# A new order for the pieces of v, q and k in a two-layer graph kernel, and a start rearranged around the graph's turning

The kernel runs on one core of a Trainium2 chip. The metric is the device time of one execution in microseconds (us).

## The reference, cut to what matters

There are 32 graphs with 512 nodes and 512 features each. All share one 0/1 adjacency matrix `adj` of 512 x 512.

```python
# layer 0
a, deg = adj.astype(x.dtype), adj.sum(axis=1)
out = deg[None, :, None] * (x @ Wi.T + b) + a @ (x @ Wj.T)
x = layernorm(x + out)
# layer 1: 8 heads of 64, scores masked where adj == 0
q, k, v = heads(x @ Wq.T + bq), heads(x @ Wk.T + bk), heads(x @ Wv.T + bv)
attn = softmax(where(adj == 0, -inf, q @ k.T / 8))
x = layernorm(x + merge(attn @ v) @ Wo.T + bo)
```

## The kernel before

The products named here are fp32. Each 512 x 512 product is made with seven quarter-size products in place of eight, called *pieces*. The pieces fall into three groups, {1, 2}, {6, 7, 4} and {5, 3}; those of a group add up in one PSUM tile of one bank. There are two such banks for the pieces, `mma` and `mmb`, with one buffer each. After every piece another engine reads the tile out (an *eviction*), so the next piece on that bank must wait for the eviction:

```python
    def piece(kind, b, i, bank):
        g = GROUP[i]
        first = (kind, b, g) not in OPEN
        if first:
            OPEN[kind, b, g] = mm_tile(bank)
        pm = OPEN[kind, b, g]
        # ... 8 matmuls (16 in layer 0) from a ring of weight blocks into pm
        prefetch()
        if i == 1:
            p1 = OPEN[kind, b, "p1"] = work([P, 2, Q], "p1", 3)
            nc.scalar.copy(p1, pm)                              # L363
        # ...
        elif kind == "v":
            if i == 2:
                nc.scalar.copy(d, pm)
            elif i in (6, 7, 4):
                nc.vector.tensor_tensor(d, pm, p1, op=OP.add)   # L382
            elif i != 1:
                nc.vector.tensor_tensor(d, d, pm, op=OP.add)    # L384
        # ... q and k likewise, L390 (two rows at once) and L399 (two parts)
```

The order of the pieces of one graph in layer 1 is a list, in which v runs on bank a, q on bank b and k on bank a:

```python
        res += [norm[0], norm[1], z(apply, n, 1), pc("v", n, 1, "a"), pc("q", n, 1, "b")]
        # ...
        res += [norm[2], norm[3], z(combos, TH, n, h, (1, 2)), pc("v", n, 2, "a"), pc("q", n, 2, "b"),
                pc("k", n, 1, "a"), z(combos, TH, n, h, (3, 4)), z(add_bo, n, 0), z(add_bo, n, 1), pc("k", n, 2, "a")]
        # ...
        for i in ORDER[2:]:                       # 6, 7, 4, 5, 3
            res += [pc("v", n, i, "a"), pc("q", n, i, "b")]
```

`combos` makes sums of quarters of the activations on GpSimd. A period (one for each graph) is this list together with layer 0 of the next graph and the attention of the graph before, cut into 8 steps. Each step begins with `scores` and `values` and, in every second step, `sums`; then its share of the pieces follows. The partial sums of the exponentials (`presum`) go out behind the first piece of a step:

```python
            late = [(presum, hp, half)]           # half 0: GpSimd, half 1: two adds on VectorE (L422)
            for f in PERIODS[n][step]:
                # ... run(f), then late and a share of the softmax's remaining work
            for g in late + extra:
                g[0](*g[1:])
```

The weights' own sums are made once, at the start, by `combine`; they are written to DRAM, from where the ring of 12 blocks reads them:

```python
    combine("wj", nc.gpsimd)
    combine("wi", nc.vector)
    prefetch()
    for f in PERIODS[0]:
        run(f)
```

`fold` puts the bias of v, times Wo, into the bias of the output: 8 matmuls, in the middle of the first period.

## Time and profile before

| | before |
|---|---|
| time, median of 3 runs | 4021.6 us (4021.29 to 4022.62) |
| span of the profiled execution | 4021.7 us |
| TensorE busy | 3876.8 us (96%) |
| length of a steady period | 122.53 us |
| graph's last block cast, first piece, first scores | 10.99, 46.02, 143.20 us |

The start, timeline of the kernel before (columns: start in us, duration in us, engine, line and operation, output <- input, shape, count; in brackets the idle time just before and what ended it):

```profile
10.99 0.43 DVE L149 CAST big<-big 128x512 f32<-128x512 int32 x1 [0.52 <-DMA big<-in_adj_dram]
...
46.02 3.62 PE L356 MATMUL mma<-ring,big 128*128 128x256 f32 x16
52.66 6.61 PE L356 MATMUL mmb<-ring,big 128*128 128x256 f32 x16 [3.02 <-POOL big L325]
...
143.20 1.99 PE L408 MATMUL sc<-q,k 64*128 64x512 f32 x8
```

The cast is when the graph has arrived in full, the second line the first piece of layer 0, the last the first scores, at which the steady schedule begins. The third shows TensorE at its lower clock: 16 matmuls take 6.61 us there, at a mean granted clock of 0.56, and 3.62 us one line above.

### The profile page before, as it was taken

What the parts mean: (1) busy time and instruction counts of PE and PEld (TensorE: products, weight loads), DVE (VectorE), ACT (ScalarE), POOL (GpSimd) and SP (SyncE); (2) the same over time, 40 slices, a digit from 0 to 9 for tenths busy, and PEclk for the clock granted to TensorE, in tenths of its full rate; (3) what the DMA queues carried; (4) which work ended last, traced back from release to release, by engine and by line L of the source; (5) the groups of instructions that cost most, each with busy time, mean ns of one, the idle gap of its engine ahead of it and who ended that gap; (6) DMA issues with size and microseconds to landing.
All of it is one profiled execution on the core that took longest, in us unless ns stands there. A gap on an engine that the chain in (4) does not pass through costs nothing.

```text
span 4021.7 us, 47158 instructions
## 1 busy us (share of the span) xinstructions
PE 3876.8 (96%) x17418; PEld 2655.3 (66%) x17418; DVE 2608.9 (65%) x3524; ACT 1059.7 (26%) x1483; POOL 1851.6 (46%) x1866
## 2 busy tenths in 40 slices
PE   6999999999999999999999999999999999999997
PEld 4766666666666666666666666666666666666663
DVE  4466666666666666666666666666666666676666
ACT  1212222222222223222222222232222222222222
POOL 3445445445345454454453454444444534544432
PEclk8999999999999999999999999999999999999998
DMA  7333343333333333333333333333333334333330
GB/s 251 103 99 106 108 121 100 103 108 110 110 115 92 113 108 103 122 100 103 108 113 108 118 89 112 109 107 116 105 98 113 107 110 118 95 106 112 105 107 22
DMA packets 284346, 437.55 MB, mean 109 GB/s; under 512 B 23248, under 2 KB 121040, under 8 KB 284112
## 3 DMA queue, kind: packets, MB, share of 16 engines
q1 hardware_dynamic: 283856, 433.94, 35.9%
q8 instruction: 142, 2.33, 0.2%
q0 software_dynamic: 256, 0.53, 0.1%
q14 instruction: 92, 0.75, 0.1%
HBM read 392.96 MB, written 41.42 MB: 108 GB/s over the span
## 4 chain that ended last, share of the span: by engine, by line
PE 81%; DVE 14%; issue 3%; ACT 1%; POOL 1%; DMA 0%; SPq 0%; POOLq 0%; ACTq 0%; DVEq 0%
PE mma L356 32%; PE mmb L356 17%; PE sc L408 10%; PE ov L430 10%; PE mmb L280 6%; DVE xh L293 5%; DVE rl L443 3%; PE ov L437 2%; DVE es L422 2%; DVE e L413 2%; PE sc L273 1%; PE sc L301 1%; DVE ov L448 1%; ACT big L302 0%; ACT p L363 0%
## 5 line engine op out<-in xcount | busy, mean ns | idle before, releaser
L356 PE MATMUL mma<-ring,big 128*128 128x256 f32 x5288 | 1228.1, 382 | 47.3 <-issue 29.3
L356 PEld LDWEIGHTS mma<-ring,big 128*128 128x128 f32 x5288 | 991.6, 190 | 236.4 <-issue 66.3
L412 ACT ACTIVATE sc<-sc 128x1024 f32<-128x1024 f32 x512 | 492.8, 1006 | 1563.2 <-PE sc L408 1562.1
L413 DVE TENSOR_TENSOR e<-sc,edge 128x1024 f32<-128x1024 f32 x512 | 602.4, 1217 | 355.9 <-ACT sc L412 355.9
L419 POOL TENSOR_TENSOR es<-e 128x1024 f32<-128x1024 f32 x128 | 301.0, 2352 | 778.4 <-PE ov L437 778.4
L325 POOL TENSOR_TENSOR big<-big 128x512 f32<-128x512 f32 x384 | 525.0, 1390 | 236.5 <-DVE big L274 196.8
L408 PE MATMUL sc<-q,k 64*128 64x512 f32 x2048 | 509.7, 616 | 0.2 <-ACT big L302 0.2
L430 PE MATMUL ov<-e,v 128*64 128x512 f32 x2048 | 497.5, 607 | 6.5 <-DVE told L448 6.5
L443 DVE RECIPROCAL rl<-ov 128x128 f32<-128x128 f32 x512 | 458.7, 927 | 5.4 <-PE ov L437 1.6
L356 PE MATMUL mma<-big,ring 128*128 128x256 f32 x1792 | 430.2, 383 | 24.6 <-ACT p L363 20.9
L248 POOL TENSOR_SCALAR mv<-mv 128x1 f32<-128x1 f32 x256 | 79.2, 309 | 774.6 <-DVE mv L247 759.8
L356 PE MATMUL mmb<-big,ring 128*128 128x256 f32 x1792 | 432.6, 384 | 0.0
L356 PEld LDWEIGHTS mmb<-big,ring 128*128 128x128 f32 x1792 | 333.1, 190 | 113.9 <-issue 47.9
L356 PEld LDWEIGHTS mma<-big,ring 128*128 128x128 f32 x1792 | 334.8, 190 | 110.5 <-ACT p L363 33.4
L430 PEld LDWEIGHTS ov<-e,v 128*64 128x64 f32 x2048 | 124.7, 136 | 347.5 <-issue 272.8
L422 DVE TENSOR_TENSOR es<-es,e 128x1024 f32<-128x1024 f32 x256 | 313.5, 1225 | 4.4
L408 PEld LDWEIGHTS sc<-q,k 64*128 64x128 f32 x2048 | 176.5, 186 | 209.4 <-issue 195.8
L371 POOL TENSOR_TENSOR xh<-xh,p 128x512 f32<-128x512 f32 x189 | 235.5, 1274 | 104.5 <-ACT p L363 103.8
L374 DVE TENSOR_TENSOR xh<-xh,mma 128x512 f32<-128x512 f32 x189 | 127.8, 676 | 232.4 <-PE mma L356 232.4
L356 PE MATMUL mmb<-ring,big 128*128 128x256 f32 x1080 | 267.3, 392 | 10.7 <-POOL big L325 8.0
L183 POOL TENSOR_TENSOR xlo<-xh,xhi 128x512 fp32r<-128x512 f32 x128 | 162.6, 1281 | 220.8 <-ACT xhi L182 220.7
L356 PEld LDWEIGHTS mmb<-ring,big 128*128 128x128 f32 x1080 | 203.9, 194 | 90.7 <-POOL big L325 33.1
(109 smaller groups left out, 3667.0 us busy)
## 6 DMA issues: line engine op xcount, KB each, us to landing
ring<-wi SPq DMA_DIRECT2D x160, 256.0 KB, 2.6
ring<-wj SPq DMA_DIRECT2D x160, 256.0 KB, 2.8
ring<-wv SPq DMA_DIRECT2D x160, 256.0 KB, 2.7
ring<-wq SPq DMA_DIRECT2D x160, 256.0 KB, 2.7
ring<-wk SPq DMA_DIRECT2D x160, 256.0 KB, 4.4
ring<-wo SPq DMA_DIRECT2D x155, 256.0 KB, 2.6
xh<-in_x_dram SPq DMA_DIRECT2D x32, 1024.0 KB, 5.5
out_dram<-xh SPq DMA_DIRECT2D x31, 1024.0 KB, 5.1
```

The lines of the kernel that those rows point to most:

```text
L280: nc.tensor.matmul(pm, parts[w][:, jc, :], adjR[:, jc, :], start=(w == 0 and jc == 0), stop=(w == 1 and jc == NC - 1))
L293: nc.vector.scalar_tensor_tensor(y, b0_r, deg_c[:, ic:ic + 1], y, op0=OP.mult, op1=OP.add)
L325: nc.gpsimd.tensor_tensor(dst, p, q, op=OP.subtract)
L356: nc.tensor.matmul(pm[:, c * Q:(c + 1) * Q], lhs, rhs, start=first, stop=(kc == 1 and n == len(terms) - 1), skip_group_check=True)
L371: nc.gpsimd.tensor_tensor(d, d, p1, op=OP.add)
L408: nc.tensor.matmul(ps[:, s, :], KT[b, hp // 2][r, hp % 2, kc * P:(kc + 1) * P], QT[b, hp // 2][r, hp % 2, :], start=True, stop=True)
L412: nc.scalar.activation(ps, ps, AF.Exp, scale=QSCALE)
L413: nc.vector.tensor_tensor(e, ps, edge[:, kc:kc + 1, :].to_broadcast([P, 2, N]), op=OP.mult)
L419: nc.gpsimd.tensor_add(ES[hp], E[0], E[1])
L422: nc.vector.tensor_add(ES[hp], ES[hp], E[kc])
L430: nc.tensor.matmul(PV[hp][s * HD:(s + 1) * HD, :], V[b][:, kc, c0:c0 + HD], E[kc][:, s, :], start=(kc == 0), stop=(kc == NC - 1))
L443: nc.vector.reciprocal(rl[:, c], pl[:, c])
```

## The change

It intends two things. First, v, q and k get an order in which no piece follows one on its own bank, so that every eviction has a piece on the other bank to hide behind. Secondly, the start is rearranged: the weights' loads go behind the turning (transposing) of the graph, on ScalarE's queue, those of wi, wj and wk in halves; `combine` is split in parts that are placed among the first graph's work; `fold` moves to the end of the first period. The bias adds of the output (`add_bo`) also move to other places in a period. Not in the cut below: the first two graphs get another order of the pieces of layer 0 (their second and third change places), and the work that makes the masks from the graph (`graph_forms`) is split in three. The core of the diff:

```diff
-    combine("wj", nc.gpsimd)
-    combine("wi", nc.vector)
-    prefetch()
-
-    for f in PERIODS[0]:
+    for i, f in enumerate(PERIODS[0]):
+        if f[1] is piece and ring.used == 0:
+            load_w(wo, woT, nc.scalar)
+            W["wo"] = [wo[:, 0:2, :], wo[:, 2:4, :]]
+            load_x(1)
+            prefetch()
         run(f)
...
-    def combine(name, eng):
+    def combine(name, eng, part):
...
-        nc.scalar.mul(n22, a22, -1.0)
+            eng.tensor_scalar(n22, a22, -1.0, 1.0, op0=OP.mult, op1=OP.mult)
...
+            if n == 0 and i == 0:
+                res += [z(combine, "wj", nc.gpsimd, 0)]
+            if n == 0 and i == 2:
+                res += [z(combine, "wi", nc.vector, 0), z(combine, "wi", nc.vector, 1)]
...
+        if n == 0:
+            res += [z(combine, "wj", nc.gpsimd, 1)]
+        if n == 1:
+            res += [z(fold)]
...
-        res += [norm[2], norm[3], z(combos, TH, n, h, (1, 2)), pc("v", n, 2, "a"), pc("q", n, 2, "b"),
-                pc("k", n, 1, "a"), z(combos, TH, n, h, (3, 4)), z(add_bo, n, 0), z(add_bo, n, 1), pc("k", n, 2, "a")]
+        res += [pc("v", n, 2, "a"), norm[2], norm[3], z(combos, TH, n, h, (1, 2)), pc("k", n, 1, "a"),
+                z(combos, TH, n, h, (3, 4)), pc("q", n, 2, "b"), pc("k", n, 2, "a")]
...
-            res += [pc("v", n, i, "a"), pc("q", n, i, "b")]
+            res += [pc("q", n, i, "b"), pc("v", n, i, "a")]
```

More of the change, by code (lines that the diff above doesn't have):

```diff
@@ L128, in gnn_attention_kernel, with load_halves @@
     load_x(0)
+    W = {}
+    def load_halves(name, src, tag, eng):
+        W[name] = [work([P, 2, D], tag, 3) for _ in range(2)]
+        for j in range(2):
+            eng.dma_start(W[name][j], rows(src)[:, 2 * j:2 * j + 2, :])
     ident = const.tile([P, P], FT, name="ident")
@@ L134, in gnn_attention_kernel @@
     nc.gpsimd.memset(mhalf, -0.5)
-    W = {}
-    W["wj"] = load_w(big(), wjT, nc.sync)
-    W["wi"] = load_w(big(), wiT, nc.sync)
-    W["wv"] = load_w(work([P, NC, D], "v", 2), wvT, nc.sync)
-    W["wq"] = load_w(work([P, NC, D], "v", 2), wqT, nc.sync)
     b0_r = load_row("b0_r", b0)
@@ L159, in gnn_attention_kernel @@
     adjT = turned(adj_f, big())
-    W["wk"] = load_w(big(), wkT, nc.sync)
-    W["wo"] = load_w(wo, woT, nc.sync)
-    load_x(1)
+    load_halves("wi", wiT, "k", nc.scalar)
+    load_halves("wj", wjT, "oT", nc.scalar)
     deg_r = const.tile([P, N], FT, name="deg_r")
@@ L191, in gnn_attention_kernel, with graph_forms @@
     ahead(0)
+    for name, src in (("wv", wvT), ("wq", wqT)):
+        t = load_w(work([P, NC, D], "v", 2), src, nc.scalar)
+        W[name] = [t[:, 0:2, :], t[:, 2:4, :]]
+    load_halves("wk", wkT, "q", nc.scalar)
     edge = const.tile([P, NC, N], BF, name="edge")
-    def graph_forms():
-        nc.vector.tensor_tensor(adj_f, adjT, adjR.bitcast(FT), op=OP.not_equal)
-        nc.vector.reduce_sum(told[:, B * HP:], adj_f.rearrange("p c i -> p (c i)"), axis=AX.X)
-        nc.vector.tensor_scalar(told[:, B * HP:], told[:, B * HP:], 2.0 * SAFE, None, op0=OP.mult)
-        nc.vector.tensor_scalar(edge, adjT, 0.0, None, op0=OP.not_equal)
+    def graph_forms(part):
+        if part == 0:
+            nc.vector.tensor_tensor(adj_f, adjT, adjR.bitcast(FT), op=OP.not_equal)
+        elif part == 1:
+            nc.vector.reduce_sum(told[:, B * HP:], adj_f.rearrange("p c i -> p (c i)"), axis=AX.X)
+            nc.vector.tensor_scalar(told[:, B * HP:], told[:, B * HP:], 2.0 * SAFE, None, op0=OP.mult)
+        else:
+            nc.vector.tensor_scalar(edge, adjT, 0.0, None, op0=OP.not_equal)
     RING = 12
@@ L207, in ring_tile @@
         return work([P, 2, Q], "ring", RING)
-    def combine(name, eng):
+    def combine(name, eng, part):
         w = W[name]
-        a11, a12, a21, a22 = [w[:, 2 * j:2 * j + 2, Q * i:Q * i + Q] for i in range(2) for j in range(2)]
-        s1, s2, s3, s4, n22 = [t[:, c].rearrange("p (c i) -> p c i", c=2)
-                               for t in [work([P, 2, N], "e", 4) for _ in range(3)] for c in range(2)][:5]
-        eng.tensor_tensor(s1, a21, a22, op=OP.add)
-        eng.tensor_tensor(s2, s1, a11, op=OP.subtract)
-        eng.tensor_tensor(s4, a12, s2, op=OP.subtract)
-        eng.tensor_tensor(s3, a11, a21, op=OP.subtract)
-        nc.scalar.mul(n22, a22, -1.0)
-        for i, t in ((6, s2), (7, s3), (4, n22), (5, s1), (3, s4)):
+        a11, a12, a21, a22 = [w[j][:, :, Q * i:Q * i + Q] for i in range(2) for j in range(2)]
+        t = [work([P, 2, N], "e", 4) for _ in range(2 - part)]
+        t = [u[:, c].rearrange("p (c i) -> p c i", c=2) for u in t for c in range(2)]
+        if part == 0:
+            s1, s2, s4 = t[:3]
+            eng.tensor_tensor(s1, a21, a22, op=OP.add)
+            eng.tensor_tensor(s2, s1, a11, op=OP.subtract)
+            eng.tensor_tensor(s4, a12, s2, op=OP.subtract)
+            made = ((6, s2), (5, s1), (3, s4))
+        else:
+            s3, n22 = t
+            eng.tensor_tensor(s3, a11, a21, op=OP.subtract)
+            eng.tensor_scalar(n22, a22, -1.0, 1.0, op0=OP.mult, op1=OP.mult)
+            made = ((7, s3), (4, n22))
+        for i, u in made:
             WS[name, i] = dram.tile([P, 2, Q], FT, name=f"{name}_{i}")
-            nc.sync.dma_start(WS[name, i], t)
+            nc.sync.dma_start(WS[name, i], u)
     for name, src in (("wi", wiT), ("wj", wjT), ("wv", wvT), ("wq", wqT), ("wk", wkT), ("wo", woT)):
@@ L231, in prefetch @@
     def prefetch():
-        while len(TILES) < min(len(KEYS), ring.used + RING):
+        while len(TILES) < min(len(KEYS), ring.used + RING) and KEYS[len(TILES)] in WS:
             t = ring_tile()
@@ L481, in phase_a @@
             res += k[i:i + 1] + g[i:i + 1]
-            if n == 0 and i == 3:
-                res += [z(graph_forms)]
-            if i == (3 if n == 0 else 1) and g:
+            if n == 0 and i == 0:
+                res += [z(combine, "wj", nc.gpsimd, 0)]
+            if n == 0 and i == 2:
+                res += [z(combine, "wi", nc.vector, 0), z(combine, "wi", nc.vector, 1)]
+            if i == 1 and g:
                 res += [z(combos, TX, n, lambda j, m: quarter(XD[n], j, m), (1,)),
@@ L509, in phase_b @@
             res = []
-            for i, bank in ALONE:
-                if n == 0:
-                    res += [z(combine, *f) for f in {6: (("wv", nc.vector),), 2: (("wq", nc.vector),),
-                                                     5: (("wk", nc.vector),)}.get(i, ())]
+            side = [z(graph_forms, i) for i in range(3)] + [z(combine, name, nc.vector, i) for name in ("wv", "wq")
+                                                            for i in range(2)] if n == 0 else [z(add_bo, 0, i) for i in range(2)]
+            for i, bank in (ALONE[0:1] + ALONE[2:3] + ALONE[1:2] + ALONE[3:]):
                 res.append(pc("l0", n, i, bank))
@@ L516, in phase_b @@
                     res += [z(stats, n, 0)]
+                res += side[:1]
+                side = side[1:]
             return res + [z(apply, n, 0), z(stats, n, 1)]
@@ L529, in phase_b @@
                 res.append(z(apply, n, 0))
+            if i in (7, 4):
+                res.append(z(add_bo, n - 1, int(i == 4)))
         return res
@@ L536, in phase_c @@
         h = lambda j, i: quarter(HT[n], j, i)
-        res = [z(fold)] if n == 0 else []
-        res += [norm[0], norm[1], z(apply, n, 1), pc("v", n, 1, "a"), pc("q", n, 1, "b")]
+        res = [norm[0], norm[1], z(apply, n, 1), pc("v", n, 1, "a"), pc("q", n, 1, "b")]
         if m >= 0:
             res += [z(stats, m, 1)]
-        res += [norm[2], norm[3], z(combos, TH, n, h, (1, 2)), pc("v", n, 2, "a"), pc("q", n, 2, "b"),
-                pc("k", n, 1, "a"), z(combos, TH, n, h, (3, 4)), z(add_bo, n, 0), z(add_bo, n, 1), pc("k", n, 2, "a")]
+        if n == 0:
+            res += [z(combine, "wk", nc.vector, 0)]
+        res += [pc("v", n, 2, "a"), norm[2], norm[3], z(combos, TH, n, h, (1, 2)), pc("k", n, 1, "a"),
+                z(combos, TH, n, h, (3, 4)), pc("q", n, 2, "b"), pc("k", n, 2, "a")]
+        if n == 0:
+            res += [z(combine, "wk", nc.vector, 1)]
         if m >= 0:
@@ L545, in phase_c @@
         for i in ORDER[2:]:
-            res += [pc("v", n, i, "a"), pc("q", n, i, "b")]
-            if i == 5 and n + 1 < B and n > 0:
-                res += [z(load_x, n + 1)]
+            res += [pc("q", n, i, "b"), pc("v", n, i, "a")]
+            if i == 5 and n + 1 < B:
+                res += [z(load_x, n + 1)] if n > 0 else []
+        if n == 0:
+            res += [z(combine, "wo", nc.vector, 0), z(combine, "wo", nc.vector, 1)]
         if n + 1 < B:
@@ L553, in fold @@
     def fold():
-        combine("wo", nc.vector)
         pd = mm_tile("b")
@@ L559, in fold @@
             nc.vector.tensor_scalar(bv_w[:, dc, :], ones, bv_c[:, dc:dc + 1], None, op0=OP.mult)
-            nc.tensor.matmul(pd, bv_w[:, dc, :], W["wo"][:, dc, :], start=(dc == 0), stop=(dc == DC - 1))
+            nc.tensor.matmul(pd, bv_w[:, dc, :], W["wo"][dc // 2][:, dc % 2, :], start=(dc == 0), stop=(dc == DC - 1))
         nc.vector.tensor_add(bo_r, bo_r, pd)
@@ L578, in last_steps @@
         own = [(4 * GA, last_part, hp, 0) for hp in range(3)]
-        return [[z(last_load), p[0], FLUSH] + c, [p[1], p[2]], [p[3], p[4]], [p[5], p[6], z(stats, m, 0), z(stats, m, 1)],
+        return [[z(last_load), p[0], FLUSH] + c + [z(add_bo, B - 1, 0), z(add_bo, B - 1, 1)], [p[1], p[2]], [p[3], p[4]], [p[5], p[6], z(stats, m, 0), z(stats, m, 1)],
                 [FLUSH, own[0], z(apply, m, 0), z(apply, m, 1), z(store, m)], [own[1]], [FLUSH, own[2]], []]
@@ L588, in last_load @@
     def last_load():
-        W["wo"] = load_w(work([P, NC, D], "xh", 3), woT, nc.sync)
+        t = load_w(work([P, NC, D], "xh", 3), woT, nc.sync)
+        W["wo"] = [t[:, 0:2, :], t[:, 2:4, :]]
     def last_part(hp, half):
@@ L598, in last_part @@
         for ic in range(2 * half, 2 * half + 2):
-            nc.tensor.matmul(ACC[ic], OT[B - 1, hp // 2][:, hp % 2, ic * P:(ic + 1) * P], W["wo"][:, hp, :],
+            nc.tensor.matmul(ACC[ic], OT[B - 1, hp // 2][:, hp % 2, ic * P:(ic + 1) * P], W["wo"][hp // 2][:, hp % 2, :],
                              start=(hp == 0), stop=(hp == HP - 1))
```

## The prediction

> **What bounds the kernel now.** I read the page first (busy shares), then TensorE's waits over the span, then the timeline of one period in the middle, then the first 146 us.
>
> ```profile
> PE 3876.8 (96%) x17418; PEld 2655.3 (66%) x17418; DVE 2608.9 (65%) x3524; ACT 1059.7 (26%) x1483; POOL 1851.6 (46%) x1866
> ```
>
> TensorE is the bound. All its idle time is 4021.7 - 3876.8 = 145 us (3.6%), so a change that takes no matmul away can't gain more than that. Idle by stretch (a table of windows): about 39 us in the first 120 us, 32 us in the last 122 us, and 2.4 us in each period of 122.5 us between (980.8 of 1000 us busy), one period for each of the 32 graphs. The waits that make up those 2.4 us:
>
> ```profile
> PE mma L356 <- issue: 29.3, 30, 1.0
> PE mma L356 <- ACT p L363: 20.9, 31, 0.7
> PE mma L356 <- DVE v L382: 9.4, 29, 0.3
> PE mma L356 <- ACT big L302: 7.2, 30, 0.3
> PE mmb L356 <- DVE oT L453: 5.1, 30, 0.3
> ```
>
> Five waits, once per period. The timeline shows what each is (the pieces before 1066 are v1, q1, v2, then k1, k2, v6; those after are q4, v5):
>
> ```profile
> 1042.64 1.99 PE L356 MATMUL mma<-ring,big 128*128 128x256 f32 x8 [0.24 <-ACT big L302]
> 1044.47 1.89 PE L356 MATMUL mmb<-big,ring 128*128 128x256 f32 x8
> ...
> 1046.42 0.56 ACT L363 COPY p<-mma 128x512 f32<-128x512 f32 x1
> ...
> 1047.07 1.97 PE L356 MATMUL mma<-ring,big 128*128 128x256 f32 x8
> ...
> 1055.44 1.89 PE L356 MATMUL mma<-big,ring 128*128 128x256 f32 x8
> ...
> 1058.00 1.99 PE L356 MATMUL mma<-big,ring 128*128 128x256 f32 x8 [0.68 <-ACT p L363]
> ...
> 1060.97 1.97 PE L356 MATMUL mma<-ring,big 128*128 128x256 f32 x8 [0.98 <-issue]
> ...
> 1072.74 2.48 DVE L422 TENSOR_TENSOR es<-es,e 128x1024 f32<-128x1024 f32 x2
> ...
> 1075.14 0.68 DVE L382 TENSOR_TENSOR v<-mma,p 128x512 f32<-128x512 f32 x1
> ...
> 1075.88 1.99 PE L356 MATMUL mma<-ring,big 128*128 128x256 f32 x8 [0.32 <-DVE v L382]
> ```
>
> Undisturbed pieces start 1.73 us apart. k1, k2 and v6 all use bank a in turn: k2 starts 2.56 us after k1 and v6 2.97 us after k2, so those two waits cost 0.83 + 1.24 us. v5 waits for v4's eviction, which stands behind the 2.4 us of L422: start to start 2.22, so 0.49. With about 0.1 us of refill after a wait the three cost some 2.8 us a period.
>
> **The Trainium skill.** "PSUM — Partial Sum Buffer", section "PSUM bank collisions raise a hardware error", says to guard PSUM by bank, not by address: so a piece on a bank waits until the last reader of it is done, as the 0.68 above shows. "SBUF — State Buffer", section "Who interferes with whom": a VectorE instruction with two SBUF inputs contends with a GpSimd instruction that reads SBUF. The trace agrees: L293 takes 1.69 us each while GpSimd combines (6.76 for four), L325 likewise rises from 1.27. "TensorE: Matmul & The Clock Gate", section "What's actually happening": after about 3.4 us idle the clock halves. The trace agrees: PEclk 0.50 from 26 to 40 us and again at 88 to 92. "DMA: Bandwidth & Descriptors", section "Issuing engines are not separate DMA queues": moving loads to ScalarE's queue saves issue time, not transfer time; here 385 GB/s is moved from 10 to 32 us, so only the order of the bytes can help.
>
> **The new order, by steps.** A period is cut in 8 steps; each begins with scores (1.92 us), values (1.87) and in every second step sums (0.86). Adding up the weights in the schedule gives where the cuts fall. Before: ...N0 N1 v1 q1 N2 N3 v2 | q2 k1 k2 v6 q6 v7 | q7 v4 q4 v5 q5 v3 | q3 k6 g0 k7 g1 (N: the transposes of the normed rows, g: gather). After: ...N0 N1 v1 q1 v2 | N2 N3 k1 q2 k2 q6 v6 q7 | v7 q4 v4 q5 v5 q3 | v3 k6 g0 k7 g1.
> Step 4 (of 1 to 8): v2 now comes right after q1 and must wait for the copy of v1, which ScalarE can't start before 1046.42, behind a norm that waits on GpSimd. Start of that copy + 0.64 (as for k2: 1057.36 to 1058.00) = 1047.06: v2 starts where it does now, and the 0.88 us of N2 and N3 that filled the gap is left for later. 0.
> Step 5: it loses 0.83 + 1.24 + 0.1 of waits and takes in N2, N3: -2.15 + 0.88 = -1.27 us. q6's combinations on GpSimd should be done 1 us early.
> Step 6: q5 now follows q4 in bank b, whose two-part eviction (0.88) stands behind the same L422: it ends 9.69 us into the step where q5 could start at 9.07, so 0.68 instead of 0.49: +0.19.
> Step 7: **v3 and k6 are both on bank a and adjacent**, which the change of order within the pairs makes. The last period shows such a pair, k6 then k7:
>
> ```profile
> 3908.16 1.99 PE L356 MATMUL mma<-big,ring 128*128 128x256 f32 x8
> 3910.94 1.99 PE L356 MATMUL mma<-big,ring 128*128 128x256 f32 x8 [0.79 <-DVE k L390]
> ```
>
> Start to start 2.78 against 1.73: +1.05.
> Sum: -1.27 + 0.19 + 1.05 = -0.03 us a period; 29 periods, -1 us. The waits are moved more than removed. The bias adds (L307, 4 x 1.24 us of GpSimd) move to a stretch where GpSimd idles 15 us (1133 to 1148): 0.
> Period 1: v2 no longer waits on the two exponentials' multiplies (1.13 + 0.47, "DVE e L413"), k2's wait (0.83) and v3's on v5 (0.50 there, 0.66 start to start) go; l0's second piece now follows the first on bank a (+0.95), v3-k6 appears (+1.05), and q3 waits on q5 (+0.7): -1.6 - 0.83 - 0.66 + 2.7 = -0.4.
>
> **The start.** Two large gaps of TensorE now:
>
> ```profile
> 36.63 2.07 PE L280 MATMUL mmb<-adjR,xhi 128*128 128x512 f32 x4 [14.55 <-ACT big L286]
> ...
> 86.69 6.64 PE L560 MATMUL mmb<-xh,big 128*128 128x512 f32 x8 [5.51 <-DVE big L559]
> ```
>
> The first is ScalarE held by a negation (L219) that waits for a buffer; the change gives that negation to the combining engine, so it goes. The graph's last block is in at A = 11.0 us; with one load of 1 MB queued behind it in place of five I put A at 8. From A I follow GpSimd and the sync queue: turning 4.1, degree sums 2.8, split and first gather to A+12; then xlo (1.3), wj's first part (3 x 1.5), xlo, two combos to A+23; wi's second part waits for wj's writes and holds the fourth gather's multiply to A+24.5; six combos beside L293 take 9 us (8.95 in a steady period), to A+33.5; wj's last part 2.5, to A+36. The sync queue takes its work in order, so x1 (1 MB, 2.7 us) and the first ring tiles come only then: the first piece starts near A+43 = 51, against 46.0 now: **+5**.
> From the first piece to v1: now 48.5 us (46.0 to 94.5) with the fold in it. After: 7 pieces x 3.45 = 24.2, a cold clock 1.7, two bank waits (1 then 2 on a, 6 then 7 on b) 1.9, norm and copy 3.2 = 31: **-17.5**. v1 to the scores without the fold: 48.7 both: 0.
> The fold now ends the period: its VectorE tiles stand behind the last k eviction (1.0) and four L293 (6.3), so TensorE idles 7.4, goes cold, and the 8 matmuls take 6.6 as now: **+14**.
> Sum +5 - 17.5 + 14 = +1.5 us. At the end: 0.
> Total: -1 - 0.4 + 1.5 = 0, so about 4022. I put the median a little lower, at **4018**, since the chain on GpSimd and the fold may be shorter than I have them.
>
> **Rivals.** (1) The order works as meant: the waits of k2, v6 and v5 go and nothing comes in their place, 2.8 x 29 = 81 us less, 3940. For it: the waits are there in every period. Against: v3-k6 is adjacent in the list itself, and VectorE is as late as now in step 6. (2) The start gains 15 to 20 us (first piece at 42, fold hidden): about 4003. For it: 14.5 us of a named gap do go. Against: the sync queue stays behind wj's last part. (3) GpSimd becomes the bound of the first stage, or the moved bias adds delay the norm's small operations: 5 to 12 us more, 4030. For it: GpSimd has 19 whole-row operations before the first piece. (4) The loads were hidden anyway and all is as before: 4022.
>
> **Range and chances.** The steady part is good to 0.3 us a period, so 9 us; the start to 8 us; together some 13 us each way: 4000 to 4032. Over 2% faster needs below 3941, more than half of all of TensorE's idle time: 0.015. Over 2% slower needs 80 us more: 0.01. Within 2%: 0.975.
>
> **What would show it.** In the waits of the changed kernel: "ACT p L363" stays once a period but at v2 (0.7 to 0.9), the 1.0 of "issue" is gone, a new wait of about 0.8 on VectorE's v3 add, and one of about 0.5 on a q eviction in place of v4's; the period stays within 122.2 to 122.8 us. The first piece starts between 47 and 54 us; before the first scores there is a gap of 5 to 8 us ended by the fold's VectorE tile. A period near 120 us, or a first piece before 44 us, would prove me wrong.

## The result, and the profile after

| | before | after |
|---|---|---|
| median | 4022.1 us (4 runs, 4021.3 to 4023.6) | 4024.7 us (4 runs, 4024.1 to 4026.3) |
| span of the profiled execution | 4021.7 us | 4024.5 us |
| graph's last block cast | 10.99 | 10.59 |
| first piece | 46.02 | 55.77 |
| first scores | 143.20 | 151.41 |
| steady period | 122.53 us | 122.45 us |

The ratio is 1.0007, with a 95% interval from 0.9989 to 1.0024: the same. Ratios here are the mean time of one kernel's fast runs over that of the other's of the same rounds, so they are not quite the ratio of the medians that are quoted. All outputs are right.

The page of the changed kernel has the same picture at the top:

```profile
PE 3872.3 (96%) x17418; PEld 2653.4 (66%) x17418; DVE 2618.5 (65%) x3529; ACT 1059.2 (26%) x1477; POOL 1856.2 (46%) x1867
```

TensorE's waits over the span (us in total, times, longest) show what the new order did:

```profile
PE mma L372 <- DVE v L400: 24.2, 31, 0.8
PE mma L372 <- DMA ring<-in_wiT_dram: 23.3, 1, 23.3
PE mma L372 <- ACT p L379: 21.1, 31, 0.7
PE mmb L372 <- DVE q L415: 15.3, 30, 0.5
...
PE mmb L589 <- DVE big L588: 7.4, 1, 7.4
PE mma L372 <- ACT big L318: 6.9, 29, 0.2
...
PE mmb L372 <- DVE oT L469: 4.9, 30, 0.2
```

The 1.0 of "issue" and the 0.3 on v4's eviction are gone. In their place are waits on L400 (the add of v3, before k6) and on L415 (q4's eviction, before q5), and the 0.7 on L379 now stands before v2. The two waits with a count of 1 belong to the start. The timeline of a period in the middle shows how each of the three arises:

```profile
1049.40 2.48 DVE L438 TENSOR_TENSOR es<-es,e 128x1024 f32<-128x1024 f32 x2
1049.47 1.20 POOL L264 TENSOR_SCALAR mv<-mv 128x1 f32<-128x1 f32 x1
...
1050.75 1.53 POOL L265 TENSOR_TENSOR mv<-mv,mhalf 128x1 f32<-128x1 f32 x1
...
1051.45 1.89 PE L372 MATMUL mmb<-big,ring 128*128 128x256 f32 x8
...
1052.69 0.81 ACT L269 ACTIVATE xh<-xh,mv 128x512 f32<-128x512 f32 x1 [1.92 <-POOL mv L266]
1052.78 0.19 POOL L264 TENSOR_SCALAR mv<-mv 128x1 f32<-128x1 f32 x1
...
1053.41 0.56 ACT L379 COPY p<-mma 128x512 f32<-128x512 f32 x1
...
1054.02 1.99 PE L372 MATMUL mma<-ring,big 128*128 128x256 f32 x8 [0.68 <-ACT p L379]
...
1078.40 2.47 DVE L438 TENSOR_TENSOR es<-es,e 128x1024 f32<-128x1024 f32 x2
1079.32 1.89 PE L372 MATMUL mma<-ring,big 128*128 128x256 f32 x8
1080.79 0.87 DVE L415 SCALAR_TENSOR_TENSOR q<-mmb,bq_c,p 128x256 f32<-128x256 f32 x2
...
1081.72 1.99 PE L372 MATMUL mmb<-big,ring 128*128 128x256 f32 x8 [0.51 <-DVE q L415]
...
1091.74 1.99 PE L372 MATMUL mma<-ring,big 128*128 128x256 f32 x8
1093.77 0.69 DVE L400 TENSOR_TENSOR v<-v,mma 128x512 f32<-128x512 f32 x1 [2.10 <-PE mma L372]
...
1094.51 1.99 PE L372 MATMUL mma<-big,ring 128*128 128x256 f32 x8 [0.78 <-DVE v L400]
```

Read from the top: while VectorE adds the exponentials (L438, two inputs from SBUF), the two tiny operations of the norm on GpSimd take 1.20 and 1.53 us; the same operations take 0.19 us (at 1052.78) and 0.55 us where VectorE isn't at L438. The norm's ACTIVATE waits for them, the copy of v1 stands behind that ACTIVATE on ScalarE, and v2 waits for the copy. In the second block, q4's eviction stands behind L438, and q5 waits for it. In the third, v3 and k6 are neighbours on bank a, and k6 waits for v3's eviction, which starts as soon as it can.

The start of the changed kernel:

```profile
10.59 0.43 DVE L152 CAST big<-big 128x512 f32<-128x512 int32 x1 [0.83 <-DMA big<-in_adj_dram]
...
35.75 11.13 POOL L341 TENSOR_TENSOR big<-big 128x512 f32<-128x512 f32 x6 [1.63 <-DVE big L290]
46.84 1.26 POOL L233 TENSOR_TENSOR e<-oT 128x512 f32<-128x512 f32 x1
48.08 0.61 POOL L234 TENSOR_SCALAR e<-oT 128x512 f32<-128x512 f32 x1
...
48.13 0.91 SPq L238 DMA_DIRECT2D wj<-e  x2
49.09 0.46 SPq L107 DMA_DIRECT2D xh<-in_x_dram  x1
49.60 0.57 SPq L250 DMA_DIRECT2D ring<-in_wiT_dram  x1
...
139.13 6.24 DVE L309 SCALAR_TENSOR_TENSOR xh<-b_r,deg_c,xh 128x512 f32<-128x512 f32 x4
...
145.72 5.77 PE L589 MATMUL mmb<-xh,big 128*128 128x512 f32 x8 [7.42 <-DVE big L588]
151.41 1.99 PE L424 MATMUL sc<-q,k 64*128 64x512 f32 x8
```

The six combinations keep GpSimd until 46.84, then it makes wj's last two sums (L233, L234). The sync queue must write those to DRAM and issue the load of x before it may issue the first block of the ring, at 49.60. Its data are there 6.2 us later; the 1 MB of x and the next blocks move in the same time. So TensorE, idle for 23.3 us, has its first piece at 55.77. At the other end the fold waits 7.42 us for its VectorE tile, which stands behind the four adds of L309, and then runs at the lower clock (5.77 us for matmuls that take 3.60 in run 8).

An account by stretch: first scores +8.2 us, period 1 -0.7, the 30 later periods -3.8 together (29 steady ones -0.09 each, the last one -1.15), what follows them -0.9; +2.8 in all, the difference of the spans.

### The profile page after: what moved, and what is told of

Same layout as the page of the kernel before. It is cut to its first block, busy times and chain, and to the rows that moved or that the text cites. A ratio compares the mean times of both kernels' runs of the same rounds, so it can differ in the third digit from the quotient of the medians.

```text
span 4024.5 us, 47060 instructions
## 1 busy us (share of the span) xinstructions
PE 3872.3 (96%) x17418; PEld 2653.4 (66%) x17418; DVE 2618.5 (65%) x3529; ACT 1059.2 (26%) x1477; POOL 1856.2 (46%) x1867
## 4 chain that ended last, share of the span: by engine, by line
PE 75%; DVE 17%; POOL 4%; issue 2%; ACT 2%; DMA 0%; SPq 0%; ACTq 0%; DVEq 0%; POOLq 0%
PE mma L372 31%; PE mmb L372 15%; PE sc L424 10%; PE ov L446 9%; PE mmb L296 6%; DVE xh L309 5%; DVE e L429 3%; DVE rl L459 3%; PE ov L453 2%; DVE es L438 2%; POOL mv L265 2%; PE sc L289 1%; POOL mv L264 1%; PE sc L317 1%; ACT sc L428 1%
## 5 line engine op out<-in xcount | busy, mean ns | idle before, releaser
L372 PE MATMUL mma<-ring,big 128*128 128x256 f32 x5288 | 1233.8, 383 | 51.3 <-DMA ring<-in_wiT_dram 23.3
L372 PE MATMUL mmb<-big,ring 128*128 128x256 f32 x1792 | 426.6, 381 | 15.3 <-DVE q L415 15.3
L438 DVE TENSOR_TENSOR es<-es,e 128x1024 f32<-128x1024 f32 x256 | 326.1, 1274 | 4.4
L269 ACT ACTIVATE xh<-xh,mv 128x512 f32<-128x512 f32 x256 | 198.5, 812 | 236.9 <-POOL mv L266 221.3
```

Source lines behind the costliest of these rows:

```text
L372: nc.tensor.matmul(pm[:, c * Q:(c + 1) * Q], lhs, rhs, start=first, stop=(kc == 1 and n == len(terms) - 1), skip_group_check=True)
L438: nc.vector.tensor_add(ES[hp], ES[hp], E[kc])
```

## The experiments

The theory: the two halves of the change are independent. The order gains a few us, because each of three removed waits has a new one in its place, of nearly its size; the start costs what the order gains, because the first piece waits for GpSimd and the sync queue and the fold is on TensorE's path. The rivals: the halves act on one another; the new waits are worth nothing in themselves, as TensorE would wait elsewhere; the moved bias adds cost time in every period. The twelve runs came in four groups, each on one chip together with the kernel before, whose medians there were 4021.8 to 4022.9 us.

### 1. Each half alone

**Run 1, the order alone**: the kernel before with the new order of v, q and k and nothing else.

```diff
-        res += [norm[2], norm[3], z(combos, TH, n, h, (1, 2)), pc("v", n, 2, "a"), pc("q", n, 2, "b"), ...
+        res += [pc("v", n, 2, "a"), norm[2], norm[3], z(combos, TH, n, h, (1, 2)), pc("k", n, 1, "a"), ...
-            res += [pc("v", n, i, "a"), pc("q", n, i, "b")]
+            res += [pc("q", n, i, "b"), pc("v", n, i, "a")]
```

> The kernel before with nothing but the new order of the v, q and k pieces (and N2, N3). Theory (waits moved, not removed): the period goes from 122.53 us to 122.4 us, so 3 to 4 us less over 30 periods, some 4018 us, with the same three new waits as the changed kernel (v2 on ACT's copy 0.68, q5 on a q eviction 0.51, k6 on v3's add 0.78). Rival (the order gains its 2.8 us a period and something else in the change, such as the moved bias adds, gives it back): 3940 to 3950 us and none of the three waits.

**Run 2, the start alone**: the changed kernel with these lines in their old order, so run 1's diff turned round (`add_bo` stays where the change put it).

> The changed kernel with the old order of the v, q and k pieces, all else as changed. Theory (the start costs 8 us, the rest nothing): first scores at 150 to 152 us, period 122.5 us, 4026 to 4031 us. Rival (the start gained and the order lost): below 4018 us.

Measured: the order alone 4016.5 us (ratio 0.9985, 0.9969 to 1.0002), the start alone 4034.6 us (1.0031, 1.0014 to 1.0048). The spans differ from that of the kernel before by -8.0 and +10.3 us; their sum, +2.3, is nearly the +2.8 of the whole change. Period 1 adds up as well: -1.6 and +0.9, against -0.7. The medians say it less sharply: -6.4 and +11.7, +5.3 together, against +2.6. As each ratio has a 95% interval of some 7 us to either side, a large interaction falls, and one of a few us can't be told from noise. With the order alone the period is 122.44 us and the same three waits are there:

```profile
PE mma L356 <- DVE v L384: 24.2, 31, 0.8
PE mma L356 <- ACT p L363: 19.6, 29, 0.7
PE mmb L356 <- DVE q L399: 15.2, 30, 0.5
```

With the start alone the waits of before are back and the period is 122.54 us against 122.53, so the moved bias adds cost nothing in a steady period; this rival falls too. Its first scores come at 152.38 and its period 1 is 0.9 us longer than before. Both that and the time, 4034.6 us, lie a little above what I had expected.

### 2. Are the new waits worth their size?

**Run 3, the gather between v3 and k6.** The gather of the next graph goes between them:

```diff
-            res += k[i:i + 1] + g[i:i + 1]
+            res += g[i:i + 1] + k[i:i + 1] if n > 0 and i < 2 else k[i:i + 1] + g[i:i + 1]
```

> The changed kernel with the first two gathers ahead of the k pieces that follow them, so that v3 and k6 (both bank a) are no longer neighbours. Theory (each wait is worth its start-to-start delay, 1.05 us, and they add up): the wait on v3's add goes, nothing in its place, 30 x 1.05 = 31 us less than the changed kernel, 3993 us. Rival (the wait only moves, to the gather whose x is then not yet split): within 8 us of the changed kernel, with a new wait on the gather's xhi or xlo.

Measured: 4018.8 us (0.9991, 0.9974 to 1.0008); the period is 122.12 us, only 0.33 less than in the changed kernel and not the full 1.05. The wait on v3 is gone, but the gather has one of its own:

```profile
1090.64 2.37 POOL L435 TENSOR_TENSOR es<-e 128x1024 f32<-128x1024 f32 x1 [23.76 <-PE ov L453]
...
1092.97 2.53 POOL L186 TENSOR_TENSOR xlo<-xh,xhi 128x512 fp32r<-128x512 f32 x2
...
1094.31 1.20 PE L296 MATMUL mmb<-adjR,xlo 128*128 128x512 f32 x4 [0.46 <-POOL xlo L186]
```

The gather's low part (`xlo`) is made on GpSimd behind a sum of exponentials, and now it is needed sooner. The rival, a wait that moves, was right about this edit. **Run 6** tests whether it stands in the way for good: on top of that edit, `xlo` is issued one piece earlier, before v3, and the load of its x one pair of pieces earlier.

```diff
-            res += [pc("q", n, i, "b"), pc("v", n, i, "a")]
-            if i == 5 and n + 1 < B:
+            res += [pc("q", n, i, "b")]
+            if i == 3 and n + 1 < B:
+                res += [z(ahead, n + 1)]
+            res += [pc("v", n, i, "a")]
+            if i == 4 and n + 1 < B:
                 res += [z(load_x, n + 1)] if n > 0 else []
...
-        if n + 1 < B:
-            res += [z(ahead, n + 1)]
```

> As the run with the first gathers ahead of k6, and the split of the next graph's x put before v3 (its load one pair of pieces earlier), so that GpSimd makes xlo before the sum of exponentials. Theory (the gain of 1.05 us was lost to the gather's own wait for xlo, 0.63 us start to start, in GpSimd's queue): neither wait is left, period 121.4 us, 3993 us. Rival (something else in step 7 is as late): period over 122 us, a new wait in step 7.

Measured: 3996.4 us (0.9932, 0.9915 to 0.9948), period 121.41 us, 1.04 less than in the changed kernel. Both waits are gone. The whole size of the v3 wait could be had, once the second one was taken away with it.

**Run 4, VectorE's sums out of the way of v2 and q5.** VectorE's half of `presum` goes to the end of its step, in every second step:

```diff
-            late = [(presum, hp, half)]
+            late, last = ([(presum, hp, 0)], []) if half == 0 else ([], [(presum, hp, 1)])
...
-            for g in late + extra:
+            for g in late + extra + last:
```

> The changed kernel with VectorE's two sums of exponentials (2.4 us together) at the end of every even step instead of after its first piece. Theory: these sums are one cause of two waits, q5's (directly in VectorE's queue, 0.67 start to start) and v2's (they hold GpSimd's small norm operations, which hold ScalarE's copy of v1, 0.84); both go, with refill 1.6 us a period, 48 us less than the changed kernel, 3977 us. Rival a: v2's wait does not come from them and stays, 0.75 us a period, 4002 us. Rival b: the sums now delay the next step's multiplies, and values or sums wait: no gain.

Measured: 4213.1 us (1.0473, 1.0455 to 1.049), slower. The expectation failed. The waits of v2 and q5 did go, but in step 8 the sums now stand behind the four adds of L309:

```profile
1033.70 6.28 DVE L309 SCALAR_TENSOR_TENSOR xh<-b_r,deg_c,xh 128x512 f32<-128x512 f32 x4
...
1039.90 2.47 DVE L438 TENSOR_TENSOR es<-es,e 128x1024 f32<-128x1024 f32 x2
1042.42 1.98 PE L453 MATMUL ov<-es,ones 128*64 128x512 f32 x4 [5.77 <-DVE es L438]
1044.33 5.77 PE L372 MATMUL mma<-ring,big 128*128 128x256 f32 x16
```

TensorE waits 5.77 us for them, and then its clock is low: 16 matmuls take 5.77 us that otherwise take 3.62. The mean granted clock of this run is 0.967 against 0.992. **Run 5** moves the sums only in the two steps where the waits are, 4 and 6:

```diff
-            late = [(presum, hp, half)]
+            late, last = ([(presum, hp, half)], [])
+            if half == 1 and hp in (1, 2):
+                late, last = last, late
```

> As the run with the late sums of exponentials, but only in steps 4 and 6; step 8 keeps them early, because there they came to stand behind the 6.2 us of the degree and bias add and made the row sums wait 5.8 us. Theory (one cause of two waits): neither v2 nor q5 waits, no new wait, 1.6 us a period less than the changed kernel: period 120.85 us, 3976 us. Rival (late sums delay what comes after them in any step): over 4010 us, with waits of the row sums or the values in TensorE's list.

Measured: 3977.0 us (0.9883, 0.9867 to 0.99), period 120.72 us, 1.73 less. Of the waits of every period, these are left:

```profile
PE mma L372 <- DVE v L400: 24.2, 31, 0.8
...
PE mma L372 <- ACT big L318: 6.9, 29, 0.2
...
PE mmb L372 <- DVE oT L469: 4.9, 30, 0.2
```

The waits of v2 on L379 and of q5 on q4's eviction, 21.1 and 15.3 us in the changed kernel, are gone but for two of 0.7. So it was VectorE's sums that held both v2 and q5. In this run the norm's two operations that stand before the copy of v1 take 0.19 and 0.55 us again. The traces also show that their duration is what held v2, and not a late input: in the changed kernel the statistics of that row were done at 1048.91, before the sums began, and its three operations on GpSimd then ran one behind the other from 1049.47 to 1052.66, 3.19 us; here they take 1.19 (1037.40 to 1038.59).

### 3. Are the costs of the start what they seem?

**Run 7, the sync queue behind wj.** The first blocks of the ring, and wo, are issued before wj's last part, and x of the second graph later:

```diff
-        if f[1] is piece and ring.used == 0:
+        if f[1] is combine and f[2] == "wj" and f[4] == 1:
             load_w(wo, woT, nc.scalar)
             W["wo"] = [wo[:, 0:2, :], wo[:, 2:4, :]]
-            load_x(1)
             prefetch()
+        if f[1] is piece and ring.used == 8:
+            load_x(1)
         run(f)
```

> The changed kernel with the first seven weight blocks asked for before wj's second part is combined and written, and x of graph 1 asked for later. Theory (the first piece waits only because the sync queue takes its work in order behind GpSimd): the first piece starts at 38 to 42 us instead of 55.8; piece 7 must still wait for wj's last blocks, at about 54 us instead of 70.9; 10 to 16 us less than the changed kernel, 4009 to 4015 us. Rival (the first stage is bound by GpSimd's combinations and adds): piece 7 or the norm is as late as before, less than 4 us gained.

Measured: 4011.5 us (0.9971, 0.9955 to 0.9988). The first piece starts at 41.54 instead of 55.77, and the first scores come 14.6 us sooner. Piece 7 did not wait for wj's last blocks, as I had expected; it starts at 56.40, after 0.85 us on an eviction:

```profile
41.54 6.16 PE L372 MATMUL mma<-ring,big 128*128 128x256 f32 x16 [9.44 <-DMA ring<-in_wiT_dram]
```

**Run 8, the fold.** Its VectorE tiles are made in the part before, and its matmuls stand right behind k3, before the adds of L309:

```diff
-            res += [z(combine, "wo", nc.vector, 0), z(combine, "wo", nc.vector, 1)]
+            res += [z(combine, "wo", nc.vector, 0), z(combine, "wo", nc.vector, 1), z(fold_tiles)]
...
-        bv_w = work([P, DC, P], "big", 6)
+        bv_w = FOLD[0]
...
+        if n == 1:                 # now ahead of combos and base
+            res += [z(fold)]
```

> The changed kernel with the fold's VectorE tiles made before the gathers of graph 1 and its matmuls issued right after the last k piece, ahead of the degree and bias adds. Theory (the 7.4 us wait is the tiles' place behind those adds, and the cold clock follows from it): no gap, 8 matmuls in 3.5 us, the first scores 9 to 10 us earlier at about 142 us, 4015 us. Rival (the fold only hides another wait there): the scores are less than 4 us earlier.

Measured: 4015.1 us (0.9982, 0.9965 to 0.9998). No gap is left, and the same eight matmuls run at the full clock:

```profile
137.79 3.60 PE L596 MATMUL mmb<-xh,e 128*128 128x512 f32 x8
141.32 1.99 PE L424 MATMUL sc<-q,k 64*128 64x512 f32 x8
```

**Run 9, the graph's arrival.** I had expected the graph's last block at 8 us, and it came at 10.6. Five small loads of biases stand on GpSimd's queue beside it. With these loads issued after the first graph's split instead of before the turning:

```diff
-    b0_r = load_row("b0_r", b0)
-    ...                            # bo_r, bq_c, bk_c, bv_c likewise
     ahead(0)
     # ... loads of wv, wq, wk
+    b0_r = load_row("b0_r", b0)
+    ...
```

> The changed kernel with GpSimd's five small loads of the biases (0.53 MB in pieces of 4 to 2048 bytes, issued at 1.5 to 4.6 us) issued only after the first split of x. It is for one number, the arrival of the graph's last block, which the prediction put at 8 us and which came at 10.6. Theory (the small loads on GpSimd's queue share the engines with the graph and x): the last block is in by 7 to 8.5 us, and the dip of the transfer rate at 5 to 6 us goes. Rival (the 2 MB themselves take that long): 10 us or later as before. The whole time should hardly move, as GpSimd then spends the 3 us of issuing later: 4020 to 4027 us.

```profile
7.68 0.43 DVE L146 CAST big<-big 128x512 f32<-128x512 int32 x1 [1.65 <-DMA big<-in_adj_dram]
```

The last block is in 2.9 us sooner. This arrival scatters between traces, but the two sets are apart: 9.39 to 10.85 in the nine with the changed start and the loads early, 7.58 to 7.68 in the three with the loads late (runs 9, 11 and 12). So these loads, 0.53 MB in all, delayed the graph. The first piece starts at 54.66, 1.1 us sooner, which is within its own scatter (54.10 to 55.77 in the seven traces with this start). The trace shows where the rest went: GpSimd now issues the loads from 19.89 to 23.03, in the middle of the chain to the first piece. Its first `xlo` starts 2.79 us sooner (17.43 against 20.22), the six combinations only 1.18 (34.57 against 35.75). The time of this run (4023.3 us) is one run and proves nothing.

### 4. Together

**Run 10** is the changed kernel with the edits of runs 5, 6, 7 and 8.

> The changed kernel with the four edits that each gained (sums of exponentials late in steps 4 and 6; gathers ahead of k6 with the split before v3; weight blocks asked for early; fold ahead of the adds). Theory (they act on different waits and add up): 47.7 + 28.3 + 13.2 + 9.6 = 99 us less than the changed kernel's 4024.7, 3926 us, ratio 0.976 to the kernel before; period 119.8 us with only the two small waits (big 0.24, oT 0.17) left. Rival (they share a resource and hide each other's gains): above 3945 us.

Measured: 3922.8 us (0.9755, 0.9738 to 0.9771). Singly they gained 47.7, 28.3, 13.2 and 9.7 us on the changed kernel, 98.9 together; the measured gain is 102. They add up. The period is 119.69 us. The waits that come back in every period are down to two:

```profile
PE mma L372 <- ACT big L318: 6.9, 29, 0.2
PE mmb L372 <- DVE oT L469: 5.2, 30, 0.4
```

**Run 11** has the bias loads of run 9 late as well.

> As the run of all four, with the bias loads late as well. If the graph arrives 2 to 3 us sooner and the first piece waits on transfers, not on GpSimd, 1 to 3 us less than all four; if GpSimd's later issue takes it back, the same within 1 us.

Measured: 3917.2 us (0.974, 0.9724 to 0.9757), 2.6% faster than the kernel before and the fastest of all. The last edit gave 5.6 us where 1 to 3 were expected, and not where they were expected: the graph arrives 2.6 us sooner (7.58 against 10.17), but the first piece starts at 40.25 against 39.87 and the first scores at 126.58 against 126.30. The spans differ by 4.7: 2.8 of them are 29 steady periods of 119.59 us in place of 119.69, and 2.2 come after the last graph's first scores. Run 9 has the same 0.10 (122.35 against 122.45). No wait goes in those periods; some matmuls of the gather and the pieces beside it follow each other a little closer. Why, no run here shows.

What remains is whether the new order is needed for this, or whether the edits alone would do. **Run 12** is the same with the old order, and without the gather's edit, which has no v3-k6 pair to part there.

> The run of all five with the old order of the v, q and k pieces (and without the gather edit, which that order does not need). It asks what the new order is worth once the waits that it brought are gone. Theory: the late sums take v5's wait (0.59 us) away, the waits of k2 and v6 (2.15 us with refill) stay, so a period of about 121.9 us against 119.8, and 3978 to 3986 us. Rival (the late sums alone are the gain and the order does not matter): within 15 us of the run of all five.

Measured: 3986.5 us (0.9909, 0.9893 to 0.9926), half a us above the range, and a period of 121.78 us. Two waits of the old order stay:

```profile
PE mma L372 <- issue: 30.2, 31, 1.0
PE mma L372 <- ACT p L379: 22.3, 33, 0.7
```

So against the kernel before of their own chips the old order gains 35 us and the new one 105. The new order, with its gather edit, is worth some 69 us, 63 of them in the 29 steady periods; run 1, where the three waits that it brings are still there, gained 6.4.

## Why the prediction was right

The time fell in the range and "same" was given most of the chances. The account of the steady part was right term by term. That the total came so near is in part luck: the sum said +1.5 us for the start, -0.4 for period 1, -1 for the steady periods and 0 for the end, the traces say +8.2, -0.7, -3.8 and -0.9, so a miss of +6.7 in the start was offset by -4.0 elsewhere. The range, too, is wider than its own sum: 13 us each way of 4018 would be 4005 to 4031. Point by point:

- **The waits are moved more than removed**: right, with each of the three named at its piece. v2 starts 4.40 us after v1, where it started 4.43 after it before; q5 starts 2.40 us after v4, against 1.73 undisturbed, so it costs 0.67, where 0.68 was predicted; k6 starts 2.77 us after v3, where 2.78 was predicted. The lengths of the steps, from scores to scores in a period in the middle, confirm each term: step 4 is 13.22 us in both, step 5 went from 17.36 to 16.03 (-1.33, predicted -1.27), step 6 from 14.93 to 15.12 (+0.19, as predicted), step 7 from 14.62 to 15.69 (+1.07, predicted +1.05). Runs 5 and 6 remove the waits and gain 1.73 and 1.04 us a period. The first is the two start-to-start delays, 0.84 + 0.67, and about 0.1 of refill for each; both are more than the idle time shown (0.68 + 0.51 and 0.78).
- **The sum for a steady period**: the sign and the smallness were right; -0.03 us was -0.09, 2.6 us over the 29 steady periods; the last period, which the prediction left at 0, gave 1.15 more. The range for the period, 122.2 to 122.8, holds 122.45. Period 1 was -0.7 instead of -0.4.
- **The bias adds cost nothing**: right in the steady part, as run 2 shows (122.54 against 122.53).
- **The start**: here the sizes were off. The term "+5" for the first piece measured +9.8 (+8.1 to +9.8 over the seven traces with this start). The trace gives its parts: the graph was in at 10.6 in place of 8 (+2.6, for which the bias loads on GpSimd's queue were not counted, as run 9 shows), and the chain from there to the first piece took 45.2 us in place of 43 (the six combinations 11.1 us and not 9; from wj's last sum to the first piece 7.1, where 7 was predicted). The term from the first piece to v1 was 33.7 us in place of 31: the lower clock cost 2.8 us at the first piece (6.38 us against 3.62) and not 1.7, and the norm and its copies some 4.9 and not 3.2. In these TensorE waits 0.70 and 2.25 us, while the norm's small operations on GpSimd take up to 1.07 us beside VectorE's combinations. The fold was well sized: 7.42 of idle time (7.4 predicted), 5.77 for the matmuls (6.6). So the start cost 8.2 us (+9.8 - 14.8 + 13.2) and not 1.5 (+5 - 17.5 + 14).
- **"The chain on GpSimd and the fold may be shorter than I have them"**, the reason for the 4 us taken off the sum: wrong in direction, the chain was longer. Without it the prediction would have been 4022, nearer to the 4024.7 measured.
- **Rivals**: the first (3940) fell for the reason given against it. The second (first piece near 42) fell as well; the sync queue was indeed behind wj's last part, and run 7 has the first piece at 41.54 once it isn't. The third was half right: GpSimd did set the first piece's time (with 17 whole-row operations, not 19) and the norm waited in the start, as just said; the moved bias adds cost nothing. The fourth (all as before, 4022) has the nearest number of all, but not the mechanism: the start lost 8.2 us and the order gained some.
- **What would show it**: all the named waits were there at the sizes named. The first piece, at 55.77, was outside 47 to 54. The rule of the clock that the prediction cites fits the traces less well than it says; the last section has the numbers.

## What to carry to other kernels

When an order is changed to part two users of a buffer, list the new neighbours too, and look at when each buffer's reader can start: the gain is the old waits less the new ones, and here it was near zero until the work ahead of the readers was moved. Take the worth of a wait from start to start, not from the idle time shown; and after an edit that removes one, look for the next wait behind it before calling the edit useless. At a start, follow each queue in its order: here one late item on the sync queue held all that stood behind it, and taking the ring's blocks past it brought the first piece forward by 14.2 us (run 7).

## What the Trainium skill lacked or had wrong

- No page that I found says what a wait of TensorE costs beyond the idle time that a profile shows. In these runs 0.68 us of idle before v2 cost 0.84 from start to start (1051.45 to 1054.02, against 1.73): a piece shows 1.89 us while undisturbed ones start 1.73 apart, so 0.16 of the wait doesn't show as idle. The piece behind a wait then shows 1.99 us, 0.1 more, and taking away 0.68 + 0.51 shortened a period by 1.73.
- "DMA: Bandwidth & Descriptors", section "Issuing engines are not separate DMA queues", says that loads of all engines interleave on the same 16 DMA engines. The runs agree, but the page gives no size for small loads beside a large one: 0.53 MB on GpSimd's queue delayed the graph's last block by 2.9 us (10.59 against 7.68; 1.7 to 3.3 over all the traces).
- "SBUF — State Buffer", section "Who interferes with whom", lacked nothing here: it calls the sharing of the port pair between VectorE and GpSimd an exclusive lock, and the trace agrees. The operation of 0.19 us that starts at 1049.47 ends at 1050.67, when the first of VectorE's two adds is over (1049.40 to 1050.62); the next, of 0.55 us, takes 1.53 beside the second.
- "TensorE: Matmul & The Clock Gate", section "What's actually happening", has the clock at half after an idle window of about 3.4 us. Shorter gaps did it here: in the kernel before the granted clock is 0.50 from 24.41 us on, 2.3 us after TensorE's last matmul (22.09), and in the changed kernel a gap of 2.25 us (86.29 to 88.54) is followed by 0.50 from 88.50 to 91.91. A gap of 3.05 us (3972.35 to 3975.40, kernel before) is followed by no drop. So in these traces the length of the gap alone does not decide it.
